# Moving the stores of the fc weight sums from GpSimd's queue to SyncE's in a cross-attention block

## The chip, the cores and the metric

The kernel runs on one core of a Trainium2 chip. The metric is the device time of one execution in microseconds (us); lower is better. The work is in float32.

## The reference

One pre-norm cross-attention block over a batch of 4, with 512 query rows, 512 context rows, a width of 512, 16 heads of 32 and an inner width of 2048. Cut to what matters:

```python
x = layer_norm(hidden_states, ln1_w, ln1_b)
q = (x @ q_w + q_b)...;  k = (encoder @ k_w + k_b)...;  v = (encoder @ v_w + v_b)...
attn = softmax(where(mask, q @ k.T * scale, lowest))
hidden = (attn @ v) @ cproj_w + cproj_b + hidden_states
y = layer_norm(hidden, ln2_w, ln2_b)
y = gelu(y @ fc_w + fc_b)
return hidden + y @ proj_w + proj_b
```

## The kernel before

The attention runs in 32 steps. A step is one half (256 query rows) of one of the 16 units (a batch and a group of four heads); unit and half together are called a pair of the exchange here, numbered like the steps. A step makes scores (TensorE, "sc", L317), adds the mask and takes minima (VectorE), takes exponentials (ScalarE), turns blocks of 32 x 32 (VectorE, into "tb"), and then the exchange brings these blocks to the partitions where the product with v needs them: `copies` (L385) has GpSimd copy four blocks in place (L393) and SyncE issue twelve DMAs from "tb" to "pT" (L398). For some pairs the target is "gt" or "xe" instead of "pT". The product with v (`attend`, L401; TensorE, "av", L415) reads this target, VectorE scales the result into "oT" (L420), and this frees the target for the exchange of the next pair. From step 10 on, step p begins with the av products of pair p - 2; behind them the copies of pair p - 1 are issued, and the av products of step p + 1 read these.

The order is written by hand: each engine takes its instructions in the order of the program, and each engine that issues DMAs has a queue in that same order. Between a step's parts other work is filled in (`put(p, ...)`): projections of q, k and v for later units (L255 "acck", L267 "accq", L278 and L298 "accv"), and from step 11 on the MLP of the first batches. Weights are loaded by SyncE: `load_w` (L248) for q, k and v, two units ahead, and `load_mlp` (L589) for fc and projection weights, as slots become free.

The fc layer is multiplied in pairs of two 128-wide column blocks, by a scheme with seven products instead of eight (`fc_seven`, L646). It needs sums of the two weight blocks. For the first two batches `fc_sums` (L679) has GpSimd make them (four TENSOR_TENSOR on 128 x 256, recorded at L600 and L597): three go to a buffer "wsum" with two slots, one takes the place of a weight in its slot in "pbt". For batch 0 the sums of all eight pairs of column blocks are also stored to a DRAM buffer ("ws"), with two DMAs (L689 and L690). The last batches load the sums from there (`load_wa`, L729), from about 504 us on. These eight pairs of column blocks are called pair 0 to pair 7 of the stores.

`fc_sums` is called first in the fill of step 10, where it makes two pairs at once,

```python
    put(10, [k], norm(0, 0, 1), [v], norm(0, 2, 3), do(fc_sums), [q], t2)
```

and then in each step from 11 on, behind the av products and the exchange and ahead of the step's block; a pair is made there only if less than two are made ahead of the fc products:

```python
        for pair in due.get(p, ()):
            attend(*divmod(pair, 2))
        if p > 10:
            fc_sums()
```

Of the kernel before, what the change touches and what calls it, by code (L numbers as in the profile page):

```python
# [51 lines left out]
def xattn_block(ctx: ExitStack, tc: tile.TileContext, x, rawT, encT, mask, q_w, k_w, v_w, c_w, fc_w, p_w, vecs, rows, out):  # L52
    nc = tc.nc
# [548 lines left out]
    def a_sums(a11, a12, a21, a22, s1, s2, s3, s4, engine=None):  # L602
        add(engine or nc.vector, s1, a21, a22)
        sub(s3, a11, a21, engine)
        sub(s2, s1, a11, engine)
        sub(s4, a12, s2, engine)
# [66 lines left out]
    sums_dram = dram.tile([NP, P, 4, 2, P], F32, tag="ws", name="ws")  # L673
    fc_pairs = [(0, c) for c in range(NP)] + [(SPLIT, c) for c in range(FIRST * FQ // 2)]

    def raw_pair(b, c):
        return [S["fcw", b, 2 * c + i] for i in range(2)]

    def fc_sums():  # L679

        while count[3] < len(fc_pairs) and count[3] < count[4] + 2:
            b, c = fc_pairs[count[3]]
            if ("fcw", b, 2 * c + 1) not in S:
                return
            x, y = raw_pair(b, c)
            s = wsum[:, count[3] % 2]
            a_sums(x[:, :2], x[:, 2:], y[:, :2], y[:, 2:], s[:, 0], s[:, 1], y[:, :2], s[:, 2], nc.gpsimd)
            if b == 0:
                nc.gpsimd.dma_start(out=sums_dram[c, :, :3], in_=s)  # L689
                nc.gpsimd.dma_start(out=sums_dram[c, :, 3], in_=y[:, :2])  # L690
            S["ws", b, c] = s[:, 0], s[:, 1], y[:, :2], s[:, 2]
            count[3] += 1

# [293 lines left out]
    def C(b):  # L987
        return [(CHAIN, lambda t=t: cproj(b, t)) for t in range(NT)]
# [4 lines left out]
    def turns2(b):  # L993
        return [(TURN, lambda d=d: ln2_turn(b, d)) for d in range(ND)]
# [88 lines left out]
    def put(p, *work, before=(), mid=()):  # L1083
# [19 lines left out]
    c, t2 = C(0), turns2(0)  # L1103
# [3 lines left out]
        c[3:], stat(0, 2), x3, stat(0, 3), rs(0))  # L1107
    k, q, v = A(8)
    put(10, [k], norm(0, 0, 1), [v], norm(0, 2, 3), do(fc_sums), [q], t2)
    k, q, v = A(9)  # L1110
    put(11, [k, v], some(2), pb_(0), mid=do(lambda: y_sums(0)))
# [23 lines left out]
    c = C(2)  # L1135
# [11 lines left out]
    for p in range(2 * NW):  # L1147
        w, half = divmod(p, 2)
        if half == 0 and w and w % NG == 0:
            make_mb(w // NG)  # L1150
        run(ahead[p])
# [5 lines that stand above are left out]
        def fill(n, work=fills[p]):  # L1157
            if n or not work or work[0][0] <= CHAIN:
                run(work, CHAIN if n < 2 else None)

        block(w, half, fill, any(cost > CHAIN for cost, _ in fills[p]), mids[p])
# [6 lines left out]
    c = cproj_last()  # L1168
# [59 lines left out]
```

## Time and profile before

| | |
|---|---|
| median of 3 runs | 761.14 us (760.96 to 763.58) |
| the profiled execution's own time | 766.39 us |
| its span, from the first to the last instruction | 764.3 us |
| busy: TensorE, VectorE, ScalarE, GpSimd | 757.5, 602.0, 337.1, 334.7 us |
| stores of the weight sums | 16 DMAs, issued by GpSimd between 163.1 and 309.0 us |
| mean granted TensorE clock | 0.997 |

PE stands for TensorE's products, DVE for VectorE, ACT for ScalarE, POOL for GpSimd, SPq for SyncE's queue. A row of a timeline has the start and the length in us, the engine, the line, the operation with what it writes and reads, and how many instructions were merged; in square brackets stands the idle time before it and what ended it. For DMAs the length is that of issuing them, and the time to landing is counted from the issue. A row of a window has the busy time of the five engines with their instructions in brackets, then the granted clock, the DMA engines' share and GB/s. In a row of a line three numbers with strokes between are the least, the median and the greatest length in ns.

### The profile page before, as it was taken

How to read it: one execution, taken by the hardware profiler on the slowest of the kernel's cores; microseconds unless marked ns; L12 is line 12 of the kernel's file. 1: busy time of each engine (PE TensorE's matmuls, PEld its weight loads, DVE VectorE, ACT ScalarE, POOL GpSimd, SP SyncE). 2: the span in 40 equal slices, each digit the busy share in tenths (PEclk: the TensorE clock that was granted, in tenths of full speed). 3: DMA queues.
4: the chain of work that ended last, by engine and by line, in shares of the span. 5: the costliest groups of instructions: out<-in, count | busy, mean ns of one | idle time of the engine just before them, and what ended most of it. 6: DMA issues, size and time to landing. Idle time of an engine off the chain costs nothing.

```text
span 764.3 us, 12899 instructions
## 1 busy us (share of the span) xinstructions
PE 757.5 (99%) x4370; PEld 518.7 (68%) x4370; DVE 602.0 (79%) x1198; ACT 337.1 (44%) x766; POOL 334.7 (44%) x350
## 2 busy tenths in 40 slices
PE   9999999999989999999999999999999999999998
PEld 6655555566565545475464566458888899988997
DVE  3888999879976777887888889958877886747762
ACT  2566766565863475647753467501202221021200
POOL 1539447368653883443584444532060004303152
PEclk9999999999999999999999999999999999999999
DMA  8999889467796686765666867776724402146001
GB/s 325 341 255 243 204 207 254 111 199 196 214 251 212 194 242 169 184 184 130 167 141 179 212 194 197 171 226 212 270 97 131 163 31 90 36 133 218 1 15 42
DMA packets 60577, 134.59 MB, mean 176 GB/s; under 512 B 11312, under 2 KB 17072, under 8 KB 60384
## 3 DMA queue, kind: packets, MB, share of 16 engines
q1 hardware_dynamic: 58448, 126.73, 58.0%
q0 software_dynamic: 1920, 7.01, 2.8%
q8 instruction: 35, 0.57, 0.3%
q14 instruction: 30, 0.25, 0.1%
q10 hardware_dynamic: 144, 0.02, 0.0%
HBM read 69.23 MB, written 11.02 MB: 105 GB/s over the span
## 4 chain that ended last, share of the span: by engine, by line
PE 98%; SPq 1%; DMA 1%; issue 0%; DVE 0%; POOL 0%; POOLq 0%; DVEq 0%
PE q L646 25%; PE accp L705 11%; PE r L790 8%; PE sc L317 8%; PE av L415 8%; PE acck L255 7%; PE accq L267 7%; PE accc L455 6%; PE accv L278 5%; PE accv L298 3%; PE q1p L844 2%; PE q4p L826 2%; PE tp L166 1%; SPq L398 1%; DMA ptt<-q_w_dram 1%; PE warm L1023 1%
## 5 line engine op out<-in xcount | busy, mean ns | idle before, releaser
L327 ACT ACTIVATE ptt<-ptt,mn 128x512 f32<-128x512 f32 x256 | 181.7, 711 | 147.6 <-DVE mn L323 147.6
L323 DVE CUSTOM_DVE_ANT_0 ptt<-sc,mb 128x512 f32<-128x512 f32 x256 | 160.6, 682 | 20.1 <-PE sc L317 20.0
L335 DVE STREAM_TRANSPOSE tb<-ptt 128x1024 f32<-128x1024 f32 x128 | 153.3, 1217 | 1.0 <-ACT ptt L327 1.0
L393 POOL COPY pT<-tb 32x1088 f32<-32x1088 f32 x96 | 104.5, 1089 | 86.4 <-DMA pbt<-p_w_dram 28.0
L705 PE MATMUL accp<-pbt,gt 128*128 128x512 f32 x192 | 85.3, 596 | 0.0
L646 PE MATMUL q<-yT,gt 128*128 128x256 f32 x320 | 78.9, 380 | 0.0
L667 ACT ACTIVATE ga<-ga,vec 128x512 f32<-128x512 f32 x40 | 26.7, 714 | 93.3 <-DVE ga L600 83.5
L646 PEld LDWEIGHTS q<-yT,gt 128*128 128x128 f32 x320 | 61.0, 191 | 8.1
L705 PEld LDWEIGHTS accp<-pbt,gt 128*128 128x128 f32 x192 | 35.9, 190 | 44.6 <-issue 39.2
L317 PE MATMUL sc<-pbt 32*128 32x512 f32 x512 | 66.1, 621 | 0.0
L646 PE MATMUL q<-ys,gt 128*128 128x256 f32 x240 | 61.6, 380 | 0.0
L255 PE MATMUL acck<-xe,ptt 128*128 128x512 f32 x128 | 58.8, 603 | 0.2 <-issue 0.2
L267 PE MATMUL accq<-xe,ptt 128*128 128x512 f32 (+1 forms) x136 | 58.5, 575 | 0.0
L646 PEld LDWEIGHTS q<-ys,gt 128*128 128x128 f32 x240 | 45.7, 191 | 6.1
L600 DVE TENSOR_TENSOR ga<-q,ga 128x512 f32<-128x512 f32 (+1 forms) x60 | 36.2, 603 | 16.9 <-PE q L646 14.3
L415 PE MATMUL av<-pT,v 128*32 128x256 f32 x768 | 47.3, 387 | 2.0 <-DMA ptt<-q_w_dram 2.0
L327 ACT ACTIVATION_READ_ACCUMULATOR ptt<-ptt,mn 128x1 f32 x256 | 47.8, 187 | 0.0
L267 PEld LDWEIGHTS accq<-xe,ptt 128*128 128x128 f32 x136 | 24.9, 190 | 31.4 <-issue 23.0
L317 PEld LDWEIGHTS sc<-pbt 32*128 32x128 f32 x512 | 27.5, 187 | 26.0 <-issue 17.2
L255 PEld LDWEIGHTS acck<-xe,ptt 128*128 128x128 f32 x128 | 23.6, 192 | 31.2 <-issue 21.9
L455 PE MATMUL accc<-wc,oT 128*128 128x512 f32 x96 | 42.5, 598 | 0.0
L415 PEld LDWEIGHTS av<-pT,v 128*32 128x32 f32 x768 | 23.0, 111 | 26.2 <-issue 10.4
(219 smaller groups left out, 1265.4 us busy)
## 6 DMA issues: line engine op xcount, KB each, us to landing
pT<-tb SPq DMA_DIRECT2D x288, 136.0 KB, 2.4
pbt<-p_w_dram SPq DMA_DIRECT2D x40, 256.0 KB, 3.3
gt<-ws SPq DMA_DIRECT2D x20, 512.0 KB, 3.4
gt<-tb SPq DMA_DIRECT2D x48, 136.0 KB, 3.8
xe<-tb SPq DMA_DIRECT2D x48, 136.0 KB, 2.5
pbt<-fc_w_dram SPq DMA_DIRECT2D x24, 256.0 KB, 4.0
gt<-fc_w_dram SPq DMA_DIRECT2D x20, 256.0 KB, 3.2
ptt<-k_w_dram SPq DMA_DIRECT2D x16, 256.0 KB, 3.7
```

What stands on the lines that cost most here:

```text
L255: nc.tensor.matmul(acc, S["wk", w][:, d, :], eT[:, d, :], start=(d == 0), stop=(d == ND - 1))
L267: nc.tensor.matmul(acc, S["wq", w][:, d, :], xT[:, d, c], start=(d == 0), stop=(d == ND - 1))
L317: nc.tensor.matmul(S["sc", w, qt][h], qT[r, ts(qt, P)], kT[r, :], start=True, stop=True)
L323: nc.vector.tensor_tensor_reduce(out=s, in0=S["sc", w, qt][h], in1=S["mb", w // NG], scale=1.0, scalar=FMAX, op0=ALU.add, op1=ALU.min, acc ...
L327: nc.scalar.activation(s, s, AF.Exp, bias=mn, scale=-1.0, accum_out=S["sums", w][:, qt, h : h + 1])
L335: nc.vector.transpose(tv[:, qt % 2, 2 * k : 2 * k + 2], S["ps", w, qt, k])
L393: nc.gpsimd.tensor_copy(pT[ts(i, HD), i], tb[ts(i, HD), i])
L415: nc.tensor.matmul(av[ts(h, HD), : 2 * P].rearrange(shape, **kw), v[:, t, ts(h, HD)], p[t][h], start=(t == 0), stop=(t == NT - 1),)
L455: nc.tensor.matmul(acc, S["oT", b][:, g, ts(t, P)], wc[:, g, :], start=(g == 0), stop=(g == NG - 1))
L646: nc.tensor.matmul(o, x[:, k], y[:, k], start=(k == 0), stop=(k == 1))
L705: nc.tensor.matmul(acc, gT[q % 2][:, k, ts(t, P)], S["pw", b, q * FQ + k], start=(k == 0), stop=(k == FQ - 1))
L790: nc.tensor.matmul(r, x[:, c], w[:, c], start=(c == 0), stop=(c == NP // 2 - 1))
```

## The change

The two stores of a pair's weight sums are issued by SyncE instead of GpSimd. They have the same sources and targets, and stand at the same place in the program: behind the four sums on GpSimd, whose end SyncE waits for; in the calls from step 11 on they come right behind the twelve copies of the exchange in SyncE's queue.

```diff
             a_sums(x[:, :2], x[:, 2:], y[:, :2], y[:, 2:], s[:, 0], s[:, 1], y[:, :2], s[:, 2], nc.gpsimd)
             if b == 0:
-                nc.gpsimd.dma_start(out=sums_dram[c, :, :3], in_=s)
-                nc.gpsimd.dma_start(out=sums_dram[c, :, 3], in_=y[:, :2])
+                nc.sync.dma_start(out=sums_dram[c, :, :3], in_=s)
+                nc.sync.dma_start(out=sums_dram[c, :, 3], in_=y[:, :2])
             S["ws", b, c] = s[:, 0], s[:, 1], y[:, :2], s[:, 2]
             count[3] += 1
```

## The prediction

> **What bounds the kernel now.** I read the page first, for its busy shares and its chain.
>
> ```profile
> span 764.3 us, 12899 instructions
> PE 757.5 (99%) x4370; PEld 518.7 (68%) x4370; DVE 602.0 (79%) x1198; ACT 337.1 (44%) x766; POOL 334.7 (44%) x350
> PE 98%; SPq 1%; DMA 1%; issue 0%; DVE 0%; POOL 0%; POOLq 0%; DVEq 0%
> ...
> ws<-wsum POOLq DMA_DIRECT2D x8, 384.0 KB, 4.2
> ...
> ws<-pbt POOLq DMA_DIRECT2D x8, 128.0 KB, 4.6
> ```
>
> TensorE is busy for 757.5 of 764.3 us, and the chain that ended last is 98% TensorE. GpSimd, which the change relieves, has no share in the chain; SyncE's queue, which the change loads, has 1%, and the DMAs another 1%. So the question is where TensorE waits for a transfer, and whether the change adds or removes such a wait. The last two lines are the moved work: 8 pairs of stores, 16 DMAs, from GpSimd's queue.
>
> The only long wait of TensorE behind its start is in step 15, and the timeline of TensorE there, with the windows by granted clock and the timelines of GpSimd and of SyncE's queue just before, tells how it came about.
>
> ```profile
> 204.65 1.93 PE L415 MATMUL av<-pT,v 128*32 128x256 f32 x32
> 206.51 2.00 PE L317 MATMUL sc<-pbt 32*128 32x512 f32 x16
> ...
> 220.17 2.77 PE L415 MATMUL av<-pT,v 128*32 128x256 f32 x32 [1.98 <-DMA ptt<-q_w_dram]
> 222.87 2.80 PE L317 MATMUL sc<-pbt 32*128 32x512 f32 x16
> ```
> ```profile
> 220.20:222.90 2.70, 2.70 (x36) 1.34 (x36) 0.01 (x1) 0.74 (x1) 0.00 (x0) 0.67 1.01 357
> 222.90:225.70 2.80, 2.80 (x20) 1.14 (x17) 1.29 (x4) 0.13 (x1) 2.13 (x2) 0.71 0.96 313
> ```
> ```profile
> 215.08 0.56 POOL L689 DMA_DIRECT2D ws<-wsum  x1 [0.30 <-POOL wsum L597]
> ```
> ```profile
> 207.16 8.52 SPq L398 DMA_DIRECT2D pT<-tb  x12
> ```
>
> The av products (L415) of a pair read the twelve copies of the exchange (L398). Those copies were issued from 207.16 to 215.68; at 215.08 GpSimd began two stores. The av products then waited 1.98 us for a transfer. The page names a weight load that they do not read; I take it that the copies landed at about that time, held up by the stores. After the wait the granted clock was 0.67 and 0.71, so that av took 2.77 instead of 1.93 us and sc 2.80 instead of 2.00. The whole hole cost 1.98 + 0.84 + 0.80 = 3.62 us.
>
> **The change part by part.** *Removed from GpSimd*: 16 DMA issues, and the 0.30 us in which GpSimd waits for its own sums ahead of each pair's first one. That is some 8 x (0.30 + 0.56 + 0.54) = 11 us. Since GpSimd has 0% of the chain, I cost it at nothing, with one use: the sums that follow at once can begin earlier.
>
> *Added to SyncE*: 16 issues. No store of weight sums by SyncE is in the trace; the nearest row is that of its four stores of hidden rows to DRAM.
>
> ```profile
> L486 SPq DMA_DIRECT2D xa<-pbt x4: 327/388/669, 525.6 to 527.3; - x4
> ```
>
> I take 0.39 us for each (ends 0.33 and 0.67), so 0.8 us for a pair (0.65 to 1.35). The first store also waits for GpSimd's fourth sum, and what is queued behind it on SyncE waits with it: the weight loads (L248, L589), the input loads, and then the next step's twelve copies, which the av products of the step after wait for. What this costs is read pair by pair.
>
> *Pairs 0 and 1*, made in one call in step 10, are the dangerous ones. The call stands in that step's fill, ahead of q's load and of step 11's exchange, so that here the stores come not only behind copies but also in front of the next ones.
>
> ```profile
> 162.05 0.73 POOL L597 TENSOR_TENSOR wsum<-pbt,wsum 128x256 f32<-128x256 f32 x1
> 163.07 0.64 POOL L689 DMA_DIRECT2D ws<-wsum  x1 [0.30 <-POOL wsum L597]
> 163.73 0.54 POOL L690 DMA_DIRECT2D ws<-pbt  x1
> 164.28 0.74 POOL L600 TENSOR_TENSOR wsum<-pbt 128x256 f32<-128x256 f32 x1
> ...
> 166.60 1.05 POOL L597 TENSOR_TENSOR wsum<-pbt,wsum 128x256 f32<-128x256 f32 x1
> ...
> 169.05 4.69 POOL L393 COPY pT<-tb 32x1088 f32<-32x1088 f32 x4
> ```
> ```profile
> 158.79 0.33 SPq L248 DMA_DIRECT2D ptt<-q_w_dram  x1
> 163.18 10.26 SPq L398 DMA_DIRECT2D pT<-tb  x12
> ```
> ```profile
> 176.76 1.03 PE L646 MATMUL q<-ys,pbt 128*128 128x256 f32 x4
> 177.71 1.93 PE L415 MATMUL av<-pT,v 128*32 128x256 f32 x32
> ```
>
> Pair 0's sums end at 162.05 + 0.73 = 162.78. Pair 1's four sums ran from 164.28 to 166.60 + 1.05 = 167.65, in 3.37 us; without the two issues between they begin at about 162.86 and end at 162.86 + 3.37 = 166.2 at the latest. SyncE then issues pair 1's stores until 166.2 + 0.8 = 167.0, with some 0.1 us to see the semaphore 167.1, q's load until about 167.5, and the first copy at about 167.6 instead of 163.18: 4.4 us later. GpSimd's own four copies do not suffer, they begin some 3 us before 169.05.
>
> How long do twelve copies then take? These rows are the two kinds of case, first of copies beside GpSimd's stores and then of copies without them, by line in the two windows, and then SyncE's timeline where copies stand straight behind loads:
>
> ```profile
> L398 SPq DMA_DIRECT2D pT<-tb x12: 513/593/1575, 163.2 to 172.8; - x12
> ...
> DMA to landing us min/median/max: 3.5/4.3/5.1
> ```
> ```profile
> L398 SPq DMA_DIRECT2D pT<-tb x12: 513/590/597, 180.2 to 187.1; - x12
> ...
> DMA to landing us min/median/max: 2.4/2.4/2.6
> ```
> ```profile
> 47.36 1.84 SPq L179 DMA_DIRECT2D xe<-encT_dram  x4
> ...
> 50.26 10.20 SPq L398 DMA_DIRECT2D gt<-tb  x12
> ...
> 70.24 0.39 SPq L248 DMA_DIRECT2D ptt<-v_w_dram  x1
> 70.73 7.49 SPq L398 DMA_DIRECT2D gt<-tb  x12
> ```
>
> Beside GpSimd's stores the twelve took 10.26 us and landed after 3.5 to 5.1; alone they start within 6.9 us (180.2 to 187.1) and land after 2.4 to 2.6. Behind one or two weight loads they took 7.49 us, behind four context loads 10.20, that is 2.7 more. Here they stand behind two stores and one load, nearer to the first. Without delay the last copy starts at 167.6 + 6.9 = 174.5 and lands at 176.9; I add 1.1 us for the stores and q's load still in flight, which gives 178.0. The av products were due at 177.71, with no gap in front of them (176.76 + 1.03 = 177.79). So the wait is 178.0 - 177.7 = 0.3 us. The lower end is 0: 0.8 us of slack are left if nothing is held up. The upper end adds 2.7 us of slower issue and a landing after 5.1: 174.5 + 2.7 + 5.1 = 182.3, a wait of 4.6 us.
>
> *Pair 2*, the tightest of the others:
>
> ```profile
> 189.54 0.73 POOL L597 TENSOR_TENSOR wsum<-pbt,wsum 128x256 f32<-128x256 f32 x1
> ```
> ```profile
> 180.22 7.50 SPq L398 DMA_DIRECT2D pT<-tb  x12
> ...
> 188.46 3.15 SPq L589 DMA_DIRECT2D pbt<-p_w_dram  x2
> 193.69 7.50 SPq L398 DMA_DIRECT2D pT<-tb  x12
> ```
>
> SyncE is through with the copies at 187.72 and waits for the sums until 190.27, 2.5 us. The stores end at 191.2, q's load at 191.8, the two projection loads at 192.7. The next copies start at 193.69, released by the preceding av product and not by the queue, so nothing is late; their landing at 193.69 + 6.9 + 2.4 = 203.0 leaves 1.65 us to the av products of 204.65, which covers a backlog of transfers. Cost 0, or what a backlog of over 1.65 us would add; without that cover each us is paid.
>
> *Pairs 3 to 7*: the sums end with the copies or before, as in the last of them,
>
> ```profile
> 307.41 0.73 POOL L597 TENSOR_TENSOR wsum<-pbt,wsum 128x256 f32<-128x256 f32 x1
> ...
> 300.51 7.82 SPq L398 DMA_DIRECT2D pT<-tb  x12
> ...
> 312.40 0.34 SPq L248 DMA_DIRECT2D ptt<-k_w_dram  x1
> ```
>
> where SyncE is free at 308.33, after the sums' end at 308.14, and has nothing until 312.40. They cost 0.8 us of an idle queue. Pair 4 is the one whose stores held up the copies before step 15: on one queue they are behind those copies, so of the 3.62 us of that hole most should go in an execution that has it.
>
> *The sum.* The profiled execution took 766.39 us, 764.3 of them its span: 766.39 - 3.62 + 0.3 = 763.1. The median of the three runs is 761.14, already 5.25 below the profiled one, more than the hole is worth; so I take it (an estimate) that the median run hardly has the hole, and count nothing for it there. 761.14 + 0.3 = 761.4 us.
>
> **The rivals.** *A hole in front of step 12's av products.* SyncE waits for pair 1's sums, and step 11's copies land late by much. For it: they start 4.4 us later and had no such slack before. Against it: they no longer share the DMA engines with GpSimd's stores. It decides once the last copy lands after about 179.7, 2 us late, as the hole of step 15 shows what 2 us bring: the slower clock, 0.84 + 0.80 = 1.64 us more. With before's own spacing of the copies (163.2 to 172.8 is 9.6) the last one starts at 177.2 and lands after 2.4 to 5.1, at 179.6 to 182.3: a wait of 1.9 to 4.6, with the clock 3.5 to 6.2, so 764.7 to 767.4 us. By the Trainium skill's page "TensorE: Matmul & The Clock Gate", part 1, the clock drops only after an idle window of about 3.4 us; by that page the rival would be paid without the clock at its lower end. The trace disagrees: 1.98 us of idle were followed by 0.67.
>
> *The hole of step 15 is in the median run too, and goes.* For it: its cause as I read it is in the program's order. Against it: the median is 5.25 us below the execution that has it. 761.14 - 3.62 + 0.3 = 757.8 us.
>
> *The queue makes no difference.* The same bytes go over the same DMA engines in the same stretch, and step 11's copies, first beside the stores and now behind them, land at the same time, 177.7 at the latest; nothing is late or early: 761.1 us. The Trainium skill's page "DMA: Bandwidth & Descriptors", section "Issuing engines are not separate DMA queues", says this: issuing from several engines saves only the sequencer's time. The landings of 3.5 to 5.1 against 2.4 to 2.6 show that two queues do cost the one of them time, so I give it little.
>
> **How the numbers follow.** Forecast (a wait of 0 to 1.5 us, nothing else) 0.54, hole before step 12 0.30, hole of step 15 gone 0.09, no difference 0.07. The likeliest gives 761.4, its own range is 760.3 to 763.0 (the fastest run of before less 0.7 of scatter, and 1.5 of wait). For 8 in 10 the range reaches down to 759.8, which leaves out the third case, and up to 766.2, which takes in the greater part of the first rival: 759.8 to 766.2. A difference of 0.5%, 3.8 us, is about what a measurement of this kernel can tell from no change, so faster means below 757.3 and slower above 764.9. Faster: 0.03, the lower side of the third case. Slower: 0.30, nearly all of the first rival with a little of the forecast's tail. Same: 0.67.
>
> **What would show it.** In the profile after, SyncE's copies of step 11 start at about 167.6 and take nearer to 7.5 than to 10.3 us; GpSimd's two groups of sums follow each other without a gap; pair 2's projection loads are issued by 193; the av products of step 12 wait less than 1 us; and the wait ahead of step 15 is below 0.5 us, with a granted clock of 1.00 behind it. I am wrong if the av products of step 12 start 2 us or more after the fc products ahead of them, or if the copies of another step start after the av product that releases them is through.

## The result, and the profile after

| | before | changed |
|---|---|---|
| median of 9 executions | 761.75 us (760.96 to 763.58) | 764.53 us (763.45 to 767.97) |
| ratio, with its 95% interval | | 1.0032 (1.0018 to 1.0046) |
| again, beside the later experiments: median | 762.89 us (29 executions) | 765.72 us (6) |
| ratio, with its 95% interval | | 1.0046 (1.0032 to 1.0061) |
| span of the profiled execution | 764.3 us | 766.2 us |

The change makes the kernel slower by some 2.8 us, by 764.53 - 761.75 and by 765.72 - 762.89 alike. The forecast was 761.4 us, within 0.5% of before; the time lies in the stated range, inside 0.5%, and above the forecast case's own range of 760.3 to 763.0.

The page of the changed kernel:

```profile
PE 758.3 (99%) x4370; PEld 518.5 (68%) x4370; DVE 604.8 (79%) x1198; ACT 337.1 (44%) x766; POOL 326.2 (43%) x334
PE 96%; DMA 2%; SPq 1%; DVE 0%; issue 0%; ACT 0%; DVEq 0%
```

The sixteen stores have moved as meant: GpSimd has 334 instructions instead of 350. The chain now holds 2% of DMA instead of 1%, and VectorE's busy time has grown from 602.0 to 604.8 us, although no instruction of VectorE was changed. That growth is the first clue. These are rows of the timelines of the changed kernel (GpSimd, SyncE, VectorE, TensorE) in steps 11 and 12; PEld stands for TensorE's weight loads:

```profile
168.05 5.58 POOL L393 COPY pT<-tb 32x1088 f32<-32x1088 f32 x4
...
169.54 8.27 SPq L398 DMA_DIRECT2D pT<-tb  x12
...
168.49 1.20 DVE L597 TENSOR_TENSOR ys<-yT 128x512 f32<-128x512 f32 x1
169.79 1.39 DVE L597 TENSOR_TENSOR ys<-yT,ys 128x512 f32<-128x512 f32 x1
171.10 1.57 DVE L597 TENSOR_TENSOR yT<-yT 128x512 f32<-128x512 f32 x1
172.60 1.57 DVE L597 TENSOR_TENSOR ys<-yT,ys 128x512 f32<-128x512 f32 x1
...
179.10 1.03 PE L646 MATMUL q<-ys,pbt 128*128 128x256 f32 x4
180.07 1.93 PE L415 MATMUL av<-pT,v 128*32 128x256 f32 x32
181.93 3.79 PE L317 MATMUL sc<-pbt 32*128 32x512 f32 x16
...
184.27 0.62 PEld L317 LDWEIGHTS sc<-pbt 32*128 32x128 f32 x4 [0.44 <-DVE gt L600]
```

and these the rows of the same sums of y (VectorE) and of the same scores (TensorE) in the timelines of before:

```profile
166.14 0.92 DVE L597 TENSOR_TENSOR ys<-yT 128x512 f32<-128x512 f32 x1
167.17 1.03 DVE L597 TENSOR_TENSOR ys<-yT,ys 128x512 f32<-128x512 f32 x1
168.12 0.68 DVE L597 TENSOR_TENSOR yT<-yT 128x512 f32<-128x512 f32 x1
168.73 0.68 DVE L597 TENSOR_TENSOR ys<-yT,ys 128x512 f32<-128x512 f32 x1
...
179.58 2.00 PE L317 MATMUL sc<-pbt 32*128 32x512 f32 x16
```

Read from the top. By step 11 the changed profile runs 2.34 us later (its av products start at 163.01 instead of 160.67), which has to be taken off first. GpSimd's sums of pair 1 follow those of pair 0 without a gap (165.09 behind 165.13), and its four copies begin at 168.05, just ahead of VectorE's four sums of y. The copies took 5.58 us instead of the 4.69 of before, and the sums of y 5.7 us (168.49 to 174.17) instead of 3.3 (166.14 to 169.41). VectorE is then 2.4 us late against TensorE, and its sums of the fc products (L600) are too. Step 12's scores, which need accumulators that L600 must read first, take 3.79 us instead of 2.00: 1.79 us lost. The av products in front of them did not wait (179.10 + 1.03 = 180.13, and they start at 180.07).

The second loss comes two steps later, in the timelines of GpSimd, SyncE's queue and TensorE:

```profile
181.31 1.28 POOL L309 TENSOR_TENSOR v<-v,row 128x512 f32<-128x512 f32 x1 [7.68 <-ACT v L283]
...
194.29 0.73 POOL L597 TENSOR_TENSOR wsum<-pbt,wsum 128x256 f32<-128x256 f32 x1
...
197.87 4.47 POOL L393 COPY pT<-tb 32x1088 f32<-32x1088 f32 x4 [2.85 <-DVE oT L420]
...
195.43 1.49 SPq L690 DMA_DIRECT2D ws<-pbt  x1
...
198.53 7.74 SPq L398 DMA_DIRECT2D pT<-tb  x12
...
195.32 1.93 PE L415 MATMUL av<-pT,v 128*32 128x256 f32 x32
...
209.88 1.93 PE L415 MATMUL av<-pT,v 128*32 128x256 f32 x32 [1.02 <-DMA ws<-wsum]
...
223.35 1.93 PE L415 MATMUL av<-pT,v 128*32 128x256 f32 x32
```

GpSimd's addition to v waits for a copy of ScalarE that stands behind the late VectorE, and starts at 181.31 instead of 176.55: 2.4 us late too, and so is what follows it on GpSimd. TensorE has lost only 1.79 us by then. So pair 2's sums end at 195.02, only 0.30 us ahead of step 13's av products, where it was 0.91 before (190.27 against 191.18); SyncE has waited for them since its copies ended, then issues two stores, a q load and two projection loads, and only at 198.53 the copies that step 14's av products need, 0.66 us behind GpSimd's half of the same exchange (197.87). The av products wait 1.02 us. Step 15's av products start without a wait.

The two losses make 1.79 + 1.02 = 2.81 us, as much as the medians differ. That they agree so closely is chance: the second loss is not the same in every execution (0.35 us in the second profile below). The two spans differ by 1.9 only, because the two profiled executions differ in other ways: 2.34 us of the changed one were lost before the first moved store, and the one of before holds the hole of step 15, 3.62 us, which I take not to be in the median run.

### The profile page after: what moved, and what is told of

Its sections match the earlier page's. It is cut to its first block, busy times and chain, and to the rows that moved or that the text cites. A ratio compares the mean times of both kernels' runs of the same rounds, so it can differ in the third digit from the quotient of the medians.

```text
span 766.2 us, 12896 instructions
## 1 busy us (share of the span) xinstructions
PE 758.3 (99%) x4370; PEld 518.5 (68%) x4370; DVE 604.8 (79%) x1198; ACT 337.1 (44%) x766; POOL 326.2 (43%) x334
## 4 chain that ended last, share of the span: by engine, by line
PE 96%; DMA 2%; SPq 1%; DVE 0%; issue 0%; ACT 0%; DVEq 0%
PE q L646 25%; PE accp L705 11%; PE sc L317 8%; PE r L790 8%; PE av L415 8%; PE accq L267 7%; PE acck L255 7%; PE accc L455 6%; PE accv L278 5%; PE accv L298 3%; PE q1p L844 2%; PE q4p L826 2%; PE tp L166 1%; DMA xe<-encT_dram 1%; DMA pbt<-p_w_dram 1%; DMA ws<-wsum 0%
## 5 line engine op out<-in xcount | busy, mean ns | idle before, releaser
L317 PE MATMUL sc<-pbt 32*128 32x512 f32 x512 | 67.9, 615 | 0.0
L600 DVE TENSOR_TENSOR ga<-q,ga 128x512 f32<-128x512 f32 (+1 forms) x60 | 36.2, 603 | 17.4 <-PE q L646 14.8
L309 POOL TENSOR_TENSOR v<-v,row 128x512 f32<-128x512 f32 x16 | 20.3, 1281 | 49.2 <-ACT v L283 38.9
```

The lines of the kernel that those rows point to most:

```text
L317: nc.tensor.matmul(S["sc", w, qt][h], qT[r, ts(qt, P)], kT[r, :], start=True, stop=True)
```

## The experiments

The theories, once both profiles were read. The *collision theory*: GpSimd, freed from issuing, copies while VectorE adds, both get slower, and VectorE's lateness costs the scores of step 12 and, through pair 2's sums, the av products of step 14. The *queue theory*, the rival nearest to the prediction: SyncE's copies of step 11 go out 4 us late behind the stores of pairs 0 and 1, and that is the loss.

**Only pairs 0 and 1 on SyncE.**

```diff
-                nc.gpsimd.dma_start(out=sums_dram[c, :, :3], in_=s)
-                nc.gpsimd.dma_start(out=sums_dram[c, :, 3], in_=y[:, :2])
+                queue = nc.sync if c < 2 else nc.gpsimd
+                queue.dma_start(out=sums_dram[c, :, :3], in_=s)
+                queue.dma_start(out=sums_dram[c, :, 3], in_=y[:, :2])
```

> Only pairs 0 and 1 are stored by SyncE, pairs 2 to 7 by GpSimd as before. Collision theory (the loss before step 12's scores comes from GpSimd, which no longer issues, beginning its copies inside VectorE's sums of y): the scores of step 12 take about 3.7 us instead of 2.0 and the sums of y about 5.7 us instead of 3.3; +1.8 us against before, 763.5. Queue theory (the loss comes from step 11's twelve copies being issued 4 us later): also +1.8, but with the av products of step 12 waiting. Third: nothing of the loss belongs to these two pairs, +0.

Measured: 764.83 us against 763.34, +1.5, ratio 1.0009 (0.9991 to 1.0027); the interval does not exclude no change. TensorE's timeline shows the long scores, and the av products ahead of them without a wait:

```profile
178.63 1.93 PE L415 MATMUL av<-pT,v 128*32 128x256 f32 x32
180.49 3.82 PE L317 MATMUL sc<-pbt 32*128 32x512 f32 x16
```

The first loss belongs to these two pairs. Step 14's av products did not wait here, so the second loss needs the other pairs too.

**Only pairs 2 to 7 on SyncE**, the same edit with `c >= 2`.

> Pairs 2 to 7 are stored by SyncE, pairs 0 and 1 by GpSimd as before. If the av products of step 14 wait because pair 2's stores and the loads behind them stand in front of step 13's copies, a wait of about 1 us at those av products and +1.0 us, 762.7, less whatever the hole of step 15 costs in a median run before (0 to 1). If that wait comes only from the delay of step 12 that the first two pairs bring, +0 and no wait.

Measured: 763.36 us against 763.34, ratio 0.9998 (0.9982 to 1.0014). The timelines of GpSimd and TensorE:

```profile
189.19 0.73 POOL L597 TENSOR_TENSOR wsum<-pbt,wsum 128x256 f32<-128x256 f32 x1
...
190.83 1.93 PE L415 MATMUL av<-pT,v 128*32 128x256 f32 x32
...
204.30 1.93 PE L415 MATMUL av<-pT,v 128*32 128x256 f32 x32
```

Pair 2's sums end at 189.92, 0.91 us ahead of step 13's av products instead of 0.30, and step 14's av products do not wait. Six of the eight pairs cost nothing by themselves, within the interval; in the changed kernel the second loss follows from the first. It is a near thing, though. The copies of step 13 start on time here, but by the times at which their semaphores complete in the trace they land 3.8 to 4.9 us after their issue, instead of 2.4 to 2.6 in the kernel before. The last one lands at 204.03, 0.3 us ahead of step 14's av products; in the kernel before it was 1.6 us (203.01 against 204.65).

**Pairs 0 and 1 on SyncE, but behind step 11's copies.** This separates the two theories: SyncE's copies are on time, GpSimd's are early.

```diff
+                late.append((nc.sync if c < 2 else nc.gpsimd, c, s, y))
+                if c >= 2:
+                    store_sums()
...
         if p > 10:
+            store_sums()
             fc_sums()
```

> The stores of pairs 0 and 1 are issued by SyncE, but one step later in the program, behind step 11's copies; pairs 2 to 7 by GpSimd as before. SyncE's copies of step 11 start on time, GpSimd's are early. Collision theory: sums of y about 5.7 us, scores of step 12 about 3.7 us, +1.8 us, 763.5. Queue theory: no loss, 761.7.

Measured: 765.06 us against 763.34, +1.7, ratio 1.0017 (1.0002 to 1.0032). The timelines of SyncE's queue, GpSimd and TensorE:

```profile
164.13 7.50 SPq L398 DMA_DIRECT2D pT<-tb  x12
...
166.68 5.58 POOL L393 COPY pT<-tb 32x1088 f32<-32x1088 f32 x4
...
178.66 1.93 PE L415 MATMUL av<-pT,v 128*32 128x256 f32 x32
180.53 3.82 PE L317 MATMUL sc<-pbt 32*128 32x512 f32 x16
...
209.93 8.49 SPq L398 DMA_DIRECT2D pT<-tb  x12
...
222.51 0.85 PE L415 MATMUL av<-pT,v 128*32 128x256 f32 x12 [1.56 <-DVE gt L600]
```

SyncE's copies take 7.50 us and start on time, and the scores are as long as in the changed kernel. The queue theory falls for the first loss. (The last two rows are taken up with the last experiments.)

**Pairs 0 and 1 on SyncE, with GpSimd held after each of them**, by a small power and a small scaling on 128x4 that nobody reads:

```diff
+                if c < 2:
+                    nc.gpsimd.tensor_tensor(hold, ones, nhalf, ALU.pow)
+                    nc.gpsimd.tensor_scalar(hold, hold, 1.0, 0.0, ALU.mult, ALU.add)
```

> As with only pairs 0 and 1 on SyncE, but GpSimd computes two small operations on 128x4 (about 1.4 us in all) after each of these two pairs' sums, so that its copies begin about when they did before. SyncE's copies of step 11 are as late as in the changed kernel. Collision theory: sums of y back to about 3.3 us, scores of step 12 at 2.0 us, +0 to 0.3 us, 761.7 to 762.0. Queue theory: +1.8, 763.5.

Measured: 764.26 us against 763.34, +0.9, ratio 1.0013 (0.9996 to 1.0030). The timelines of SyncE's queue and TensorE:

```profile
168.47 8.53 SPq L399 DMA_DIRECT2D pT<-tb  x12
...
160.30 1.93 PE L416 MATMUL av<-pT,v 128*32 128x256 f32 x32
...
179.18 1.93 PE L416 MATMUL av<-pT,v 128*32 128x256 f32 x32 [1.76 <-DVE gt L601]
181.04 2.00 PE L318 MATMUL sc<-pbt 32*128 32x512 f32 x16
```

Half a miss, and a useful one. The scores are back at 2.00, as the collision theory says; but the first hold also delayed pair 1's sums and with them SyncE, so that its copies start 8.2 us behind step 11's av products instead of 6.5 (169.54 - 163.01 in the changed kernel). Step 12's av products then wait 1.76 us. The row names a sum on VectorE, but in the kernel before the same sums still ran when these av products started; I take the wait to be for the copies, the last of which lands at 178.77, 0.4 us before it ends. In the changed kernel the last copy lands at 179.57, 0.5 us before the av products start at 180.07. So the prediction's rival, late copies in front of step 12, is real and was missed by a few tenths of a microsecond.

**GpSimd held after pair 1 alone**, twice as long (about 2.8 us), pairs 0 and 1 on SyncE: now SyncE is as in the changed kernel and only GpSimd's copies are later.

```diff
+                if c == 1:
+                    for _ in range(2):
+                        nc.gpsimd.tensor_tensor(hold, ones, nhalf, ALU.pow)
+                        nc.gpsimd.tensor_scalar(hold, hold, 1.0, 0.0, ALU.mult, ALU.add)
```

> Pairs 0 and 1 on SyncE, the rest on GpSimd; GpSimd computes four small operations on 128x4 (about 2.8 us) after pair 1's sums alone, so that SyncE's stores and copies of step 11 go out as in the changed kernel and only GpSimd's copies are held back. Collision theory: sums of y at about 3.3 us, scores of step 12 at 2.0 us, the av products of step 12 start without a wait; as before, +0 to +0.3 us. Queue theory: a wait of 1.8 us at the av products or the scores of step 12, +1.8.

Measured: 762.68 us against 762.89, ratio 1.0006 (0.9990 to 1.0021). The timelines of SyncE's queue, GpSimd and TensorE, and the line of the sums of y:

```profile
166.11 8.24 SPq L399 DMA_DIRECT2D pT<-tb  x12
...
167.85 4.47 POOL L394 COPY pT<-tb 32x1088 f32<-32x1088 f32 x4
...
159.60 1.93 PE L416 MATMUL av<-pT,v 128*32 128x256 f32 x32
...
178.51 2.00 PE L318 MATMUL sc<-pbt 32*128 32x512 f32 x16
...
L598 DVE TENSOR_TENSOR ys<-yT,ys x2: 684/688/692, 165.9 to 167.1; 128x512 f32<-128x512 f32 x2
```

SyncE's copies start 6.5 us behind step 11's av products, as in the changed kernel, and cost nothing. GpSimd's copies take 4.47 us, the sums of y 0.69 us each, the scores 2.00. The first loss is shown to be the collision.

**All eight pairs on SyncE, with the same hold after pair 1.**

> All eight pairs on SyncE as in the changed kernel, with the same four small operations on GpSimd after pair 1's sums. If the wait of 1.0 us at step 14's av products follows from the collision (VectorE late, so v late, so GpSimd's bias and pair 2's sums late against TensorE), it goes together with the long scores: no wait in steps 12 to 15, +0 to +0.5 us against before and 2 us or more under the changed kernel. If it is the queue's own price, the 1.0 us stays.

Measured: 762.74 us against 762.89, ratio 1.0005 (0.9994 to 1.0017), where the changed kernel beside it had 765.72. TensorE's timeline, scores of step 12 and av products of step 14:

```profile
181.43 2.00 PE L318 MATMUL sc<-pbt 32*128 32x512 f32 x16
...
206.50 1.93 PE L416 MATMUL av<-pT,v 128*32 128x256 f32 x32
```

Both losses go when GpSimd does nothing of use for 2.8 us: the whole price of the change is the collision and what follows from it. The copies of step 13 land after 2.3 to 3.5 us here.

**Pair 2's sums 1.1 us later**, pairs 2 to 7 on SyncE, 0 and 1 on GpSimd:

```diff
+            if (b, c) == (0, 2):
+                nc.gpsimd.tensor_tensor(hold, ones, nhalf, ALU.pow)
```

> Pairs 2 to 7 on SyncE, 0 and 1 on GpSimd, and one small operation of about 1.1 us on GpSimd ahead of pair 2's sums, so that these end about 0.2 us after the av products of step 13 begin, where they ended 0.9 us before them without it and 0.3 before them in the changed kernel. If lateness of pair 2's sums makes the wait, step 14's av products wait 1.0 us or more, +1 to +2 us. If the collision acts on step 14 in another way, no wait.

Measured: 763.49 us against 762.89, +0.6, ratio 1.0004 (0.9988 to 1.0020): by time not told from no change. The timelines of GpSimd and TensorE:

```profile
189.56 0.73 POOL L598 TENSOR_TENSOR wsum<-pbt,wsum 128x256 f32<-128x256 f32 x1
...
190.16 1.93 PE L416 MATMUL av<-pT,v 128*32 128x256 f32 x32
...
204.25 1.93 PE L416 MATMUL av<-pT,v 128*32 128x256 f32 x32 [0.55 <-DMA ws<-pbt]
```

The wait of step 14 appears without any collision, once pair 2's sums end 0.13 us behind the start of step 13's av products. It is 0.55 us, less than expected; the way (late sums, SyncE held, copies late) is the one named. Its size does not follow from the lateness of the sums alone: they are later here than in the changed kernel, and the wait is shorter. What the profiles show is that SyncE's copies start 2.51 us behind step 13's av products where nothing is lost, and 0.24 us later than that here, 0.70 in the changed kernel and 0.34 in its second profile, with waits of 0.55, 1.02 and 0.35 us; and that in these three the copies land 3.5 to 5.3 us after their issue. I take the slower landing to come from the stores and loads that SyncE held back and then issued straight ahead of the copies; no run shows that by itself.

**The changed kernel again.**

> The changed kernel again beside the others: +2 to +3 us against before, the long scores of step 12 (3.7 us) and a wait at step 14's av products (about 1 us) in its profile. If the two of the first profile were chance, neither.

Measured: the ratio of 1.0046 in the table above, +2.8 us by the medians. TensorE's timeline:

```profile
179.86 3.80 PE L317 MATMUL sc<-pbt 32*128 32x512 f32 x16
...
207.15 1.93 PE L415 MATMUL av<-pT,v 128*32 128x256 f32 x32 [0.35 <-DMA ws<-wsum]
```

The long scores come back within a hundredth; the second wait is 0.35 instead of 1.02.

**Pair 4's stores three times, by GpSimd and by SyncE.** The prediction put the hole of step 15 down to pair 4's stores, issued by another queue while step 14's copies were in flight. Here these stores are tripled, the extra ones to a spare buffer.

```diff
+                for k in range(2 if c == 4 else 0):
+                    queue.dma_start(out=spare[k, :, :3], in_=s)
+                    queue.dma_start(out=spare[k, :, 3], in_=y[:, :2])
```

> Pair 4's two stores are issued three times by GpSimd (the extra ones to a spare buffer), everything else as before. If stores from another queue hold up the landing of copies already issued, the hole ahead of step 15's av products is there in most executions and larger than before's 1.98 us, 3 us or more with the slow clock behind it; +3 to +5 us. If the hole of the first profile came from elsewhere, +0 to +0.5 us.

> Pair 4's two stores are issued three times, all by SyncE behind step 14's copies; the other pairs by GpSimd. On one queue the stores are behind the copies: no hole ahead of step 15's av products (under 0.3 us), +0 to +0.5 us. If only the bytes in flight count and not the queue, the same hole as with GpSimd.

Measured against 762.87 us: by GpSimd 762.83, ratio 1.0003 (0.9993 to 1.0013); by SyncE 762.78, ratio 0.9997 (0.9977 to 1.0017). The timelines of GpSimd, SyncE's queue and TensorE with GpSimd's tripled stores, and the landing of the twelve copies:

```profile
214.96 0.56 POOL L691 DMA_DIRECT2D ws<-wsum  x1 [0.30 <-POOL wsum L597]
...
207.04 7.88 SPq L398 DMA_DIRECT2D pT<-tb  x12
...
218.00 1.93 PE L415 MATMUL av<-pT,v 128*32 128x256 f32 x32
...
DMA to landing us min/median/max: 2.3/2.4/2.7
```

No wait at step 15's av products, with three times the bytes. So the stores did not hold up copies that were already on their way. But this does not overturn the prediction's reading of the hole, because here all twelve copies were issued before the first store. The hole showed up in two profiles, before's and the one with the stores of pairs 0 and 1 behind step 11's copies, where it was 1.56 us. From the latter, GpSimd's first store and the landing of the copies:

```profile
217.84 0.56 POOL L684 DMA_DIRECT2D ws<-wsum  x1 [0.30 <-POOL wsum L597]
...
DMA to landing us min/median/max: 2.4/2.4/4.4
```

In these two the copies took 8.5 us to issue (8.52 and 8.49), so that the twelfth went out just behind the first store: by 0.01 us in before's profile (215.09), by 0.07 in the other (217.91). By the semaphores in the traces this one copy landed 4.6 and 4.4 us after its issue, at 219.71 and 222.32, and the av products started at 220.17 and 222.51. In the four other profiles in which GpSimd issues pair 4's stores, the copies took 7.75 to 8.24 us to issue, the twelfth went out 0.3 to 0.8 us ahead of the first store, and it landed after 2.5 to 3.0 us. So the hole fits a last copy that falls behind the stores. No run moved the stores to test this, and what stretches the issuing in some executions stays open.

## Why the prediction was right and wrong

*The number.* The time lies in the stated range because that range took in most of the first rival, late copies in front of step 12. That rival did not happen; something else cost about as much. That the number fits is luck.

*What was right.* The change gains nothing; nobody waited for the 11 us taken off GpSimd; SyncE's copies of step 11 start late by 4 us (6.5 us behind step 11's av products instead of 163.18 - 160.67 = 2.5) and take nearer to 7.5 than to 10.3 us (8.27); the two stores of pair 0, and those of pair 1, take some 0.75 us of SyncE (0.33 + 0.42) where 0.8 was forecast; pairs 3 to 7 cost nothing that the measurement can tell; and the median run before most likely does not hold the hole of step 15 (two of the six profiles with GpSimd's stores of pair 4 have it). That TensorE loses something in step 12 came true too, but not by the way forecast.

*The term that was sized 0.3.* The wait of step 12's av products for late copies is 0. Two of its parts stood in no row: 1.1 us for transfers still in flight, and 0.1 us to see the semaphore. The last copy landed at 179.57 - 2.34 = 177.2 in the time of before, where 178.0 was forecast and 176.9 without the 1.1; SyncE's store began 0.03 us behind the sums (168.14 against 168.11). The experiment with the longer delay shows how little slack was left: copies issued 1.6 us later (8.17 against 6.53 us behind step 11's av products), the last of them landing 1.9 us later, made 1.76 us of wait. The upper end of 4.6 let the last copy land after 5.1 us, as the ninth of before's twelve did; before's last one landed after 2.5.

*The step that failed.* "GpSimd's own four copies do not suffer, they begin some 3 us before 169.05", and ahead of it that GpSimd's relief costs nothing, "with one use". I checked who waits for GpSimd and not what runs beside it. An engine off the chain that becomes early moved its copies into VectorE's additions, and the price was 1.8 us. The rows to see it were there: in the profile before, the first two sums of y, which ran beside GpSimd's sums, took 0.92 and 1.03 us, and the two that ran almost wholly beside its issuing of stores 0.68. The Trainium skill has the rule, on its page "SBUF — State Buffer", section "Who interferes with whom": a VectorE instruction with two inputs in SBUF contends with a GpSimd instruction that reads SBUF. The trace agrees: sums of y with both inputs in SBUF went from 0.68 to 1.57 us beside GpSimd's copies.

*Pair 2* was costed at nothing with a cover of 1.65 us. That holds as long as its sums end where they did (no wait with pairs 2 to 7 on SyncE), but the cover was nearly gone even then, by a last copy that landed 3.8 us after its issue instead of 2.4. The collision moved the sums towards the next av products, and the queue behind SyncE's wait did the rest, 1.02 and 0.35 us in the two profiles. The prediction had "released by the preceding av product and not by the queue, so nothing is late", and named the contrary as a sign of being wrong. It came: SyncE's copies of step 13 start 0.66 us behind GpSimd's, which wait for the release alone, and pair 2's projection loads are through at 198.37, which is 194.2 in the time of before (less 2.34 and 1.79), and not 193. Part of that is pair 2's own two stores: they took 1.82 us of SyncE (0.33 + 1.49) and 1.49 us in the second profile (0.33 + 1.16), where 0.65 to 1.35 was allowed. The two edits of one change, each read alone, cost 1.5 to 1.8 and 0; together 2.8 by the medians. The sum of the pairs left out what one does to the other.

*The hole of step 15.* That the wait would be gone in the changed profile came true, and the reason given, stores that stand behind the copies on one queue, fits the six profiles compared above. The test with tripled stores could not show it. The first rival took 2 us of idle TensorE to bring the slower clock. Before's 1.98 us did (0.67); the waits of 1.76 and 1.56 us in two of the experiments did not, the granted clock behind them was 1.00.

No version here beats the kernel before: those without a loss lie within 0.1% of it.

## What to carry to other kernels

When an edit makes an engine earlier, look up what it will run beside at the new time, and read from the trace what the two cost each other when they overlap; "off the chain" says only that nobody waits for it. A store that waits for another engine holds everything behind it in its queue, so place it by what is queued behind it and by how late its producer can get, not by how late it was in one profile. And a wait seen in one profiled execution is not yet a cost of the median: here the faster kernel's profile held the longest wait.

## What the runs showed of the hardware

VectorE's additions of 128x512 from SBUF and GpSimd's copies of 32x1088 slow each other: 0.68 to up to 1.57 us for the one, and for four of the other 4.47 to 5.58 us. The same 4.47 us were enough for the copies when the additions had ended before.

A copy that SyncE issued 0.01 to 0.07 us behind a store of GpSimd landed after 4.6 and 4.4 us; one issued 0.3 to 0.8 us ahead of such a store landed after 2.5 to 3.0 us. An idle TensorE of 1.98 us was followed by a granted clock of 0.67, one of 1.76 or 1.56 us by 1.00.
